# A hand-written planner for a gated MLP with a quantized down projection: how its orders are made and judged

## The chip, the cores and the metric

The kernel runs on one core of a Trainium2 chip. The metric is the device time of one execution in microseconds (us).

## The reference

For four sequences of 1,024 tokens with 512 features:

```python
scale = cond @ norm_w.T + 1.0
ms = jnp.mean(x * x, axis=-1, keepdims=True)
h = x * (scale[:, None, :] * jax.lax.rsqrt(ms + EPS))
u = h @ up_w.T                       # 512 -> 4096
val, gate = jnp.split(u, 2, axis=-1)
h = val * jax.nn.gelu(gate, approximate=False)
hq = act_quant(h)                    # per token: round(h * 127/max|h|), scaled back
wq = weight_quant(down_w)            # one scale: round(w / mean|w|) to -1, 0, 1
y = hq @ wq.T                        # 2048 -> 512
return y + x
```

The inputs are `x` (4, 1024, 512), `cond` (4, 128), `norm_w` (512, 128), `up_w` (4096, 512) and `down_w` (512, 2048), all float32.

## The kernel before

**The work.** A batch is one of the four sequences. For each batch the up projection goes over 16 blocks of 128 value and 128 gate features (`j`, or `g` counted through all batches); a block is a "slot". Weights and activations are split into a high and a low half in 16 bits, so that three matmuls make one product of 32-bit quality. Batch 0 is done block by block while the weights are still being loaded, scaled, transposed and split (`first_batch`, `plain_half`; matmuls on L886; the first of them in `plain_first`, L929). The weights also go in a rearranged form to a scratch tensor in device memory (`s_dram`). Batches 1 to 3 load them from there and use seven products of half-size blocks in place of eight (`slot`, `product`, L871), six matmuls of 512 columns to a product. The results of the products are collected in PSUM banks named A (two), B (one) and E (two), copied and combined by ScalarE (ACT: L949, L957, L961, gelu on L966 and L982; in batch 0 gelu on L910) and VectorE (DVE: L969, L979, L985, L988; in batch 0 L914).

**The down projection.** When a batch is up-projected, the maximum of each token is taken (DVE: L1005, L1007; then over partitions on GpSimd, POOL: L1021), turned into a scale (DVE: L1026, L1032), and the activations are scaled and rounded in pieces (DVE: L1063, L1067; ACT: L1071, L1075) during the next batch. Its matmuls (`Pair`, L1142; for the last batch `down_mm`, L1091) run in slots 10 to 13 of the next batch. They need four sums of weight blocks (`d_sums`, L771, DVE), and end in L1182 and L1100, which add `x` before the result is stored.

**The head.** The first loads, the rsqrt of the first token rows (L1214 to L1219), their scaling (L1224 on ACT, L1226 on DVE and POOL), their transposes on TensorE (PE, L1231), a table load for gelu on ACT (L1300), the maximum of the first weight rows (L578), a small matmul that spreads the condition (L482) and matmuls that only keep PE busy (`keep_warm`, L1247) are recorded in the order of the source.

**What sets the order.** Nothing above is issued at once. `Engine` records every call as a `Step` with its engine, a price in us and the steps it depends on (`Plan.add`); dependencies come from the memory that operands share. `Plan.order` then looks for an order in 24 rounds. In each, `needed` goes backwards and gives each step the latest time at which it may end (PE's steps are tied to their starts in the round before); `place` goes through the steps by that time and puts each in the first gap of its engine that is long enough (`Line`), except PE's, which are put one after the other; `replay` runs the resulting lists, each engine in order, against the prices and returns when PE is free. The round with the earliest end gives the order, and `emit` issues it; each engine then works strictly through its own list. DMAs are issued from the SP queue, a few from ACT. `price` holds the costs: a fixed part, a part per column, and for DVE and POOL a second, higher price for when the other of the two works at the same time.

Of the kernel before, what the change touches and what calls it, by code (L numbers as in the profile page):

```python
# [97 lines left out]
class Engine:  # L98
    def __init__(self, plan, name, real):
        self._plan, self._name, self._real = plan, name, real  # L100
# [10 lines left out]
class Plan:  # L111


    def __init__(self):
        self.steps = []
        self.wrote, self.read = {}, {}
        self.loaded = {}
        self.lines = {}

    def engines(self, nc):  # L120
# [3 lines left out]
    def add(self, eng, method, real, args, kwargs):  # L124
        s = Step()
        s.n, s.eng, s.do, s.args, s.kwargs = len(self.steps), eng, real, args, kwargs
        s.line = sys._getframe(2).f_lineno
        operands = [(i == 0, a) for i, a in enumerate(args)]
        operands += [(k in ("out", "accum_out"), a) for k, a in kwargs.items()]
        operands = [(w, a) for w, a in operands if isinstance(a, bass.AP)]  # L130
        writes = [a for w, a in operands if w]
        reads = [a for w, a in operands if not w]
        s.alone, s.beside, s.wait = price(eng, method, writes, reads, args, kwargs)
        deps = set()
        for v in reads:
            name, grains = _runs(v)
            wrote, read = self.wrote.setdefault(name, {}), self.read.setdefault(name, {})
            for g in grains:
                if g in wrote:
                    deps.add(wrote[g])  # L140
                r = read.setdefault(g, [])
                if r and r[-1] == s.n:
                    continue
                if eng == "PE" and r and self.steps[r[-1]].eng == "PE":
                    r[-1] = s.n
                else:
                    r.append(s.n)
        for v in writes:
            name, grains = _runs(v)
            wrote, read = self.wrote.setdefault(name, {}), self.read.setdefault(name, {})  # L150
            for g in grains:
                if g in wrote:
                    deps.add(wrote[g])
                deps.update(read.pop(g, ()))
                wrote[g] = s.n
        kind, s.before = None, 0.0
        if method == "activation" and args[2] in (AF.Sqrt, AF.Gelu):
            kind = args[2]
        elif eng == "POOL":
            kind = method == "partition_all_reduce"  # L160
        if kind is not None:
            was, members = self.loaded.get(eng, (None, []))
            if kind != was:
                deps.update(members)
                if eng == "POOL" and members:
                    s.before = RELOAD
                members = []
            elif members:
                deps.add(members[0])
            members.append(s.n)  # L170
            self.loaded[eng] = kind, members
        deps.discard(s.n)
        s.deps = deps
        self.steps.append(s)

    def order(self):

        steps = self.steps
        for s in steps:
            s.after, s.cost = [], (s.alone + s.beside) / 2  # L180
        for s in steps:
            for d in s.deps:
                steps[d].after.append(s)
        clock = 0.0
        for s in steps:
            if s.eng == "PE":
                s.start = clock
                clock += s.cost
        best = None
        for n in range(ROUNDS):  # L190
            self.needed(clock)
            self.place()
            order = sorted(steps, key=lambda s: (s.start, s.n))
            clock = self.replay(order)
            if best is None or clock < best[0]:
                best = clock, order
        self.replay(best[1])
        return best[1]

    def needed(self, clock):  # L200

        for s in reversed(self.steps):
            s.late = clock if s.eng != "PE" else s.start
            for t in s.after:
                s.late = min(s.late, t.late - lag(s, t) - s.wait - s.cost)

    def place(self):

        steps = self.steps
        used = {e: Line() for e in ("PE", "ACT", "DVE", "POOL", "SP", "DMA")}  # L210
        last = 0.0
        for s in sorted(steps, key=lambda s: (s.late, s.n)):
            t = max((steps[d].end + lag(steps[d], s) for d in s.deps), default=0.0)
            if s.eng == "PE":
                t = max(t, last)
                last = t + s.cost
                s.start, s.end = t, last
                continue
            s.start = used[s.eng].put(t - s.before, s.before + s.cost) + s.before
            s.end = s.start + s.cost  # L220
            if s.wait:
                s.end = used["DMA"].put(s.start + ISSUE, s.wait) + s.wait + LANDING

    def replay(self, order):

        steps = self.steps
        free = dict.fromkeys(("PE", "ACT", "DVE", "POOL", "SP", "DMA"), 0.0)
        port = {"DVE": 0.0, "POOL": 0.0}
        for s in order:
            e = s.eng  # L230
            t = free[e] + s.before
            for d in s.deps:
                t = max(t, steps[d].end + lag(steps[d], s))
            cost = s.alone
            if s.beside > s.alone:
                x = port["POOL" if e == "DVE" else "DVE"] - t
                if x > 0:
                    cost += (s.beside - s.alone) * min(1.0, x / s.alone)
                port[e] = t + cost
            s.start, s.end = t, t + cost  # L240
            s.cost = (s.cost + cost) / 2 if e in port else cost
            free[e] = s.end
            if s.wait:
                free["DMA"] = max(free["DMA"], t + ISSUE) + s.wait
                s.end = free["DMA"] + LANDING
        return free["PE"]

    def emit(self, steps):
        for s in steps:
# [2 lines left out]
            call(s.do, s.args, s.kwargs)  # L252


ROUNDS, ISSUE, LANDING, RELOAD = 24, 1.2, 1.5, 6.5


class Line:
# [17 lines left out]
def lag(s, t):  # L276

    if s.eng == t.eng:
        return 0.0
    if s.eng == "PE":  # L280
        return 0.2
    return 0.08 if t.eng == "POOL" else 0.05


def price(eng, method, writes, reads, args, kwargs):

    out = writes[0]
    n = _free(out)
    if "dma" in method:
        nbytes = n * out.shape[0] * mybir.dt.size(out.dtype)  # L290
        if "transpose" in method:
            return 0.45 + nbytes / 32768 * 0.16, 0.0, nbytes / 32768 * 0.17
        last = min(v.ap[-1][1] * mybir.dt.size(v.dtype) if v.ap[-1][0] == 1 else 4 for v in (out, reads[0]))
        return 0.45, 0.0, nbytes / (290e3 if last >= 1024 else 1.5e3 if last < 64 else 150e3)
    wide = max([n] + [_free(v) for v in reads if len(v.shape) > 1])
    psum = any(str(v.space).endswith("PSUM") for v in reads)
    if eng == "PE":
        f32 = any(v.dtype == F32 for v in reads)
        return (max(n, 64) * (2 if f32 else 1) / 2.4 + 2.5) / 1e3, 0.0, 0.0
    if eng == "ACT":  # L300
        cost = 0.06 + wide * 0.0009 + (0.07 if method != "copy" else 0)
        return cost, 0.0, 0.0
    if eng == "POOL":
        if method == "partition_all_reduce":
            return (1.8 if wide > 1 else 0.4), 0.0, 0.0
        if method == "tensor_scalar":
            cost = 0.2 + wide * 0.00092
            return cost, cost * 1.2, 0.0
        cost = 0.75 if wide <= 8 else 0.18 + wide * 0.00195
        return cost, cost * 1.33, 0.0  # L310
    if method == "reciprocal":
        return 0.17 + max(0, wide - 8) * 0.0056, 0.0, 0.0
    if wide <= 32:
        return 0.17, 0.0 if psum else 0.44, 0.0
    if psum or method in ("tensor_reduce", "memset"):
        return 0.1 + wide * 0.00108, 0.0, 0.0
    if method == "tensor_scalar":
        cost = 0.1 + wide * 0.00052
        return cost, cost * 2.2, 0.0
    if method == "tensor_tensor" and all(v.dtype in (BF16, F16) for v in reads):  # L320
        cost = 0.1 + wide * 0.00052
        return cost, cost * 1.6, 0.0
    cost = 0.1 + wide * 0.00106
    return cost, cost * (1.35 if method == "scalar_tensor_tensor" else 1.65), 0.0


class Rings:
# [1550 lines left out]
```

## Time and profile before

| | |
|---|---|
| median of 3 runs (lowest to highest) | 745.54 us (744.97 to 746.1) |
| the profiled execution: time, span | 746.14 us, 744.4 us |
| PE (matmuls) busy | 725.6 us |
| DVE busy | 606.1 us |
| ACT busy | 392.7 us |
| POOL busy | 210.5 us |
| mean granted TensorE clock | 0.998 |

The span goes from the first to the last instruction; the execution's own time has some start and end around it. A matmul counts as busy until its modelled end. An engine's idle time before an instruction is put down to what released that instruction.

### The profile page before, as it was taken

The numbers are of one execution on the slowest core, as the hardware profiler recorded it, in microseconds if no ns is written. First come the engines' busy times: TensorE is split into PE (matmuls) and PEld (weight loads), VectorE is DVE, ScalarE is ACT, GpSimd is POOL, SyncE is SP. The second block draws the span as 40 slices with busy tenths as digits, with TensorE's granted clock in tenths as the row PEclk, the third lists the DMA queues.
The fourth block names the chain that finished last, engine by engine and source line by source line (L and its number), as shares of the span: only waits on it lengthen the run. The fifth ranks groups of instructions, "written<-read, shape, count | busy, mean of one in ns | idle before, by whom it ended". The sixth has DMA issues, their size and how long they took to land.

```text
span 744.4 us, 10218 instructions
## 1 busy us (share of the span) xinstructions
PE 725.6 (97%) x3684; PEld 362.5 (49%) x3684; DVE 606.1 (81%) x833; ACT 392.7 (53%) x635; POOL 210.5 (28%) x213
## 2 busy tenths in 40 slices
PE   6999999999979999999999999999999999999997
PEld 3544444444434445666444445566444444445744
DVE  6787899988988887977587888988579889755897
ACT  5787576565225688333334678623333665332363
POOL 1775887857223034300015003800001000000000
PEclk9999999999999999999999999999999999999999
DMA  9838688899423454768733454676833344443514
GB/s 305 334 87 267 226 222 220 194 248 233 139 68 99 125 138 120 176 178 193 202 101 100 100 131 124 161 199 153 192 122 102 100 103 104 107 103 89 153 48 151
DMA packets 179567, 115.74 MB, mean 155 GB/s; under 512 B 141750, under 2 KB 147767, under 8 KB 179516
## 3 DMA queue, kind: packets, MB, share of 16 engines
q1 hardware_dynamic: 179226, 114.76, 57.5%
q10 hardware_dynamic: 290, 0.33, 0.3%
q8 instruction: 29, 0.48, 0.3%
q14 instruction: 22, 0.18, 0.1%
HBM read 58.93 MB, written 23.09 MB: 110 GB/s over the span
## 4 chain that ended last, share of the span: by engine, by line
PE 78%; DVE 9%; POOL 4%; issue 3%; ACT 3%; DMA 1%; SPq 0%; DVEq 0%; POOLq 0%; ACTq 0%
PE A L871 31%; PE E L871 15%; PE po L1142 8%; PE B L871 8%; PE E L886 5%; PE B L886 2%; PE A L886 2%; PE po L1091 2%; PE E L1091 1%; PE A L1091 1%; DMA H<-in_x_dram 1%; DVE H L629 1%; POOL H L663 1%; DVE nx L854 1%; DVE wam L578 1%
## 5 line engine op out<-in xcount | busy, mean ns | idle before, releaser
L871 PEld LDWEIGHTS <-SXY 128*128 128x128 f16 x2016 | 197.3, 98 | 237.1 <-issue 5.8
L871 PE MATMUL A<-R,SXY 128*128 128x512 f16 x1152 | 266.4, 379 | 3.7 <-ACT t L949 1.6
L871 PE MATMUL E<-R,SXY 128*128 128x512 f16 x576 | 140.0, 379 | 0.8 <-DVE t L979 0.8
L1021 POOL PARTITION_ALL_REDUCE am<-R x8 | 18.9, 2364 | 304.3 <-DVE R L1007 286.4
L1063 DVE TENSOR_TENSOR H<-H,am 128x1024 f32<-128x1024 f32 x64 | 78.3, 1256 | 0.2
L886 PEld LDWEIGHTS <-SXY 128*128 128x128 f16 x462 | 45.2, 98 | 55.6 <-issue 2.1
L969 DVE SCALAR_TENSOR_TENSOR H<-A,sg,t 128x512 f32<-128x512 f32 x48 | 35.9, 749 | 43.0 <-PE A L871 42.9
L871 PE MATMUL B<-R,SXY 128*128 128x512 f16 x288 | 70.0, 379 | 0.0
L1005 DVE TENSOR_REDUCE gm<-H 128x512 f32<-128x1024 f32 x56 | 69.0, 1232 | 1.0
L982 ACT ACTIVATE t<-t,sg 128x512 f32<-128x512 f32 x48 | 34.7, 722 | 54.6 <-DVE t L979 54.6
L949 ACT COPY t<-A 128x512 f32<-128x512 f32 x48 | 28.1, 585 | 60.0 <-PE A L871 60.0
L1142 PE MATMUL po<-wd,R 128*128 128x256 fp8e4 (+1 forms) x448 | 56.8, 275 | 0.8 <-ACT po L1168 0.8
L957 ACT COPY B<-A 128x512 f32<-128x512 f32 x48 | 27.4, 570 | 51.4 <-PE A L871 51.4
L1142 PEld LDWEIGHTS <-R 128*128 128x128 bf16 (+1 forms) x480 | 47.0, 98 | 13.9 <-issue 1.3
L985 DVE TENSOR_TENSOR v<-A,v 128x512 f32<-128x512 f32 x48 | 33.2, 691 | 24.9 <-PE A L871 22.4
L966 ACT ACTIVATE t<-B,sg 128x512 f32<-128x512 f32 x48 | 33.0, 687 | 32.6 <-PE B L871 32.0
L886 PE MATMUL E<-R,SXY 128*128 128x512 f16 x210 | 49.9, 379 | 0.0
L979 DVE TENSOR_TENSOR t<-E,t 128x512 f32<-128x512 f32 x48 | 33.0, 687 | 20.4 <-PE E L871 19.7
L886 PEld LDWEIGHTS <-R 128*128 128x128 f16 x282 | 27.5, 98 | 34.4 <-issue 2.0
L1071 ACT ACTIVATE H<-H 128x1024 f32<-128x1024 f32 x38 | 40.0, 1051 | 7.5 <-DVE H L1063 7.3
L961 ACT COPY v<-E 128x512 f32<-128x512 f32 x48 | 28.1, 586 | 28.4 <-PE E L871 21.5
L1007 DVE TENSOR_TENSOR R<-R,gm 128x512 f32<-128x512 f32 x56 | 40.4, 722 | 1.4
(232 smaller groups left out, 1036.9 us busy)
## 6 DMA issues: line engine op xcount, KB each, us to landing
SXY<-s_dram SPq DMA_DIRECT2D x66, 256.0 KB, 2.7
SXY<-s_dram SPq DMA_DIRECT2D x18, 384.0 KB, 3.9
H<-in_L_cond_up_w_dram SPq DMA_DIRECT2D x13, 512.0 KB, 5.5
s_dram<-SXY SPq DMA_DIRECT2D x14, 384.0 KB, 4.0
xr<-in_x_dram SPq DMA_DIRECT2D x19, 256.0 KB, 3.7
out_dram<-xr SPq DMA_DIRECT2D x19, 256.0 KB, 2.0
H<-in_x_dram SPq DMA_DIRECT2D x8, 512.0 KB, 5.3
R<-in_L_cond_down_w_dram SPq DMA_DIRECT2D x8, 512.0 KB, 7.4
```

What stands on the lines that cost most here:

```text
L871: PE.matmul(o, s[:, w, k, :], tv[:, :, c, l, k, :], start=start and n == 0, stop=stop and n == len(TERMS) - 1, skip_group_check=True,)
L886: PE.matmul(ps, a[k // 2][:, w, k % 2, :], XP[:, l, k, h * TOK : (h + 1) * TOK], start=n == 0, stop=n == len(terms) - 1,)
L966: ACT.activation(cur["t1"], pb, AF.Gelu, scale=gain(g, 1))
L969: DVE.scalar_tensor_tensor(h_half(g - 1, 0), prev["A"], gain(g - 1, 0), prev["t1"], ALU.mult, ALU.mult)
L979: DVE.tensor_tensor(prev["t2"], prev["E"], prev["t2"], ALU.add)
L982: ACT.activation(prev["t2"], prev["t2"], AF.Gelu, scale=gain(g - 1, 1))
L985: DVE.tensor_tensor(cur["v"], cur["A"], cur["v"], ALU.add)
L1005: DVE.tensor_reduce(gm[0], v, AX.X, ALU.max, apply_absolute_value=True)
L1007: return [largest, lambda: DVE.tensor_tensor(m, m, gm[0], ALU.max)]
L1063: DVE.tensor_tensor(v, v, r.to_broadcast([P, 2, TOK]), ALU.mult)
L1071: ACT.activation(v, v, AF.Copy, bias=MAGIC)
L1142: PE.matmul(po, w[:, j], m, start=start and j == 0, stop=stop and j == n - 1, skip_group_check=True,)
```

## The change

The instructions stay the same; only the planner and its prices are changed, and with them the order in which the instructions stand in each engine's list.

- `add`: each of the first 150 recorded steps that is not a DMA also depends on the step recorded before it on its engine, so these keep their recorded order (loads are free of it). Fifty-nine of them are PE's and 57 DVE's; they end in the first matmuls of `plain_first`.
- `order`: a round's order is replayed four more times with chance, and the mean of the four ends decides between 25 rounds; the margin that `place` gets goes round from 0 to 0.9 us.
- `needed`: a step without PE behind it must start, not end, a step's cost before the end.
- `place`: PE's steps may now go into any gap that fits, like those of other engines. The other engines' steps start later than their operands allow by up to the margin, but by no more than a tenth of their slack. A DMA from SP is issued when the DMA engines have room; one from ACT takes no room.
- `replay`: with chance, the cost of each step not on PE is multiplied by 0.95 to 1.09, and a DMA from SP lands up to 1 us later. It returns the end of the last step of all, not PE's.
- `price`: ACT's reads from PSUM cost 0.05 more and its base is changed; POOL's price beside DVE rises from 1.33 to 1.42 times, DVE's beside POOL from 1.65 to 1.8.

```diff
@@ class Plan
-        self.loaded = {}
+        self.loaded, self.last = {}, {}
...
+        if not s.wait:
+            if s.n < HEAD and eng in self.last:
+                deps.add(self.last[eng])
+            self.last[eng] = s.n
...
-        best = None
+        best, chance = None, random.Random(1)
         for n in range(ROUNDS):
             self.needed(clock)
-            self.place()
+            self.place(0.3 * (n % 4))
             order = sorted(steps, key=lambda s: (s.start, s.n))
             clock = self.replay(order)
-            if best is None or clock < best[0]:
-                best = clock, order
+            late = sum(self.replay(order, chance) for _ in range(MISSES)) / MISSES
+            if best is None or late < best[0]:
+                best = late, order
+            self.replay(order)
...
-            s.late = clock if s.eng != "PE" else s.start
+            s.late = s.start if s.eng == "PE" else clock - s.cost
...
-    def place(self):
+    def place(self, margin):
...
-        last = 0.0
         for s in sorted(steps, key=lambda s: (s.late, s.n)):
             t = max((steps[d].end + lag(steps[d], s) for d in s.deps), default=0.0)
-            if s.eng == "PE":
-                t = max(t, last)
-                last = t + s.cost
-                s.start, s.end = t, last
-                continue
+            if s.eng != "PE":
+                t += min(margin, max(0.0, s.late - t) * 0.1)
+            if s.wait and s.eng == "SP":
+                t = used["DMA"].put(t + ISSUE, s.wait) - ISSUE
             s.start = used[s.eng].put(t - s.before, s.before + s.cost) + s.before
-            s.end = s.start + s.cost
-            if s.wait:
-                s.end = used["DMA"].put(s.start + ISSUE, s.wait) + s.wait + LANDING
-
-    def replay(self, order):
+            s.end = s.start + (ISSUE + s.wait + LANDING if s.wait else s.cost)
+
+    def replay(self, order, chance=None):
...
+            if chance:
+                cost *= 1.0 if e == "PE" else 0.95 + 0.14 * chance.random()
+            else:
+                s.cost = (s.cost + cost) / 2 if e in port else cost
             s.start, s.end = t, t + cost
-            s.cost = (s.cost + cost) / 2 if e in port else cost
             free[e] = s.end
-            if s.wait:
+            if s.wait and e != "SP":
+                s.end = t + ISSUE + s.wait + LANDING
+            elif s.wait:
                 free["DMA"] = max(free["DMA"], t + ISSUE) + s.wait
-                s.end = free["DMA"] + LANDING
-        return free["PE"]
+                s.end = free["DMA"] + LANDING + (chance.random() if chance else 0.0)
+        return max(s.end for s in order)
...
-ROUNDS, ISSUE, LANDING, RELOAD = 24, 1.2, 1.5, 6.5
+HEAD = 150
+ROUNDS, MISSES, ISSUE, LANDING, RELOAD = 25, 4, 1.2, 1.5, 6.5
...
-        cost = 0.06 + wide * 0.0009 + (0.07 if method != "copy" else 0)
+        cost = 0.08 + wide * 0.0009 + (0.05 if method != "copy" else 0) + (0.05 if psum else 0)
...
-        return cost, cost * 1.33, 0.0
+        return cost, cost * 1.42, 0.0
...
-    return cost, cost * (1.35 if method == "scalar_tensor_tensor" else 1.65), 0.0
+    return cost, cost * (1.35 if method == "scalar_tensor_tensor" else 1.8), 0.0
```

More of the change, by code (lines that the diff above doesn't have):

```diff
@@ L1 @@
 import bisect
+import random
 import sys
```

## The prediction

> **What bounds the kernel now.** I read the page first: the span, and how much of it each engine is busy.
>
> ```profile
> span 744.4 us, 10218 instructions
> PE 725.6 (97%) x3684; PEld 362.5 (49%) x3684; DVE 606.1 (81%) x833; ACT 392.7 (53%) x635; POOL 210.5 (28%) x213
> ```
>
> TensorE is idle for 744.4 - 725.6 = 18.8 us. The change adds and removes no instruction: set side by side, the instruction lists of the two built programs hold the same entries on each engine (7,276 on PE with its weight loads, 829 DVE, 602 ACT, 223 POOL, 362 SP), in another order. So the question is what of the 18.8 us an order can take away. That the rest is full is seen in the chain that ended last, where a group of twelve matmuls of 512 columns reads
>
> ```profile
> 229.25 2.59 PE A L871 x12
> ```
>
> 2.59 / 12 = 0.216 us each, one behind the other. The windows view then places the idle time (columns: window; its us; busy us and count of PE, weight loads, DVE, ACT, POOL; granted clock; DMA share; GB/s):
>
> ```profile
> 0.00:20.00 20.00, 13.63 (x54) 6.77 (x54) 11.98 (x56) 10.31 (x21) 2.97 (x8) 0.91 0.92 312
> ...
> 140.00:160.00 20.00, 18.27 (x85) 8.21 (x84) 17.30 (x22) 11.62 (x20) 11.25 (x13) 1.00 0.99 239
> ...
> 200.00:220.00 20.00, 17.11 (x78) 7.51 (x77) 18.89 (x25) 6.34 (x13) 3.16 (x1) 1.00 0.28 80
> 220.00:240.00 20.00, 18.44 (x86) 8.30 (x85) 15.62 (x19) 11.75 (x17) 7.91 (x8) 1.00 0.36 98
> ...
> 720.00:744.40 24.40, 20.30 (x110) 10.58 (x108) 19.65 (x27) 10.46 (x10) 0.00 (x0) 1.00 0.37 130
> ```
>
> Idle: 6.37 in the first 20 us, 1.73 at 140, 2.89 + 1.56 = 4.45 at the change from batch 0 to batch 1, 4.10 at the end; 2.1 us are scattered. The list of PE's waits says who ended them (engine, line, releaser: total, times, longest):
>
> ```profile
> PE B L886 <- ACT t L910: 1.7, 1, 1.7
> PE A L871 <- ACT t L949: 1.6, 1, 1.6
> PE A L871 <- DVE v L985: 1.2, 1, 1.2
> ...
> PE A L886 <- ACT R L1235: 0.8, 4, 0.2
> PE po L1142 <- ACT po L1168: 0.8, 2, 0.5
> ```
>
> All of it is one engine's queue standing in the wrong order for PE, never a DMA in the main part.
>
> **The change part by part.** *The change of batch, 4.45 us.* DVE's timeline there:
>
> ```profile
> 191.93 2.35 DVE L771 TENSOR_TENSOR wd<-wd 128x1024 fp8e4<-128x1024 fp8e4 x2
> ...
> 196.86 3.20 DVE L771 TENSOR_TENSOR wd<-wd 128x1024 fp8e4<-128x1024 fp8e4 x2
> ...
> 201.09 3.39 DVE L1032 RECIPROCAL am<-am 128x128 f32<-128x128 f32 x4
> ...
> 206.52 0.68 DVE L985 TENSOR_TENSOR v<-A,v 128x512 f32<-128x512 f32 x1
> ...
> 215.04 0.63 DVE L979 TENSOR_TENSOR t<-E,t 128x512 f32<-128x512 f32 x1
> ```
>
> Four weight sums (L771), 2.35 + 3.20 = 5.55 us, stand in a queue that is already full, a good ten slots ahead of their use; then 215.04 - 206.52 = 8.5 us pass from slot 0's L985 to its L979, while PE has 36 matmuls for a slot, 36 x 0.216 = 7.8 us. In the new list the four sums stand about 60 places further back, in batch 1. Between L985 and L979 the new list has the scale L1026, the four reciprocals (3.39), one L969 and one L1063:
>
> ```profile
> L1063 DVE TENSOR_TENSOR H<-H,am 128x1024 f32<-128x1024 f32 x64 | 78.3, 1256 | 0.2
> L969 DVE SCALAR_TENSOR_TENSOR H<-A,sg,t 128x512 f32<-128x512 f32 x48 | 35.9, 749 | 43.0 <-PE A L871 42.9
> ```
>
> 3.39 + 1.26 + 0.75 = 5.4, and L1026, which is a pass over 512 columns and bounded by L985's 0.68, makes at most 6.1 us: under 7.8. I followed DVE, ACT and PE in this way, by hand and with such durations, over slots 0 to 4, and found no wait over 0.1 us. One thing there is still badly priced: the maximum over partitions on POOL, for which the planner still counts 1.8 us.
>
> ```profile
> 209.17 3.16 POOL L1021 PARTITION_ALL_REDUCE am<-R  x1 [9.42 <-DVE R L1007]
> ```
>
> DVE will stand for up to 3.16 - 1.8 = 1.4 us at L1026 of the second half, with an L969 queued behind it; PE wants the bank that this L969 frees only 18 matmuls, 3.9 us, after its input is complete, so I count nothing. Bounds: gain 4.45, or 4.45 - 1.4 = 3.05. I take 4.45.
>
> *The wait at 142, 1.73 us.* ACT and POOL there:
>
> ```profile
> 142.59 0.41 ACT L674 CAST R<-H 128x256 f16<-128x256 f32 x1 [4.60 <-POOL H L665]
> 142.90 0.68 ACT L910 ACTIVATE t<-B,sg 128x512 f32<-128x512 f32 x1
> ```
>
> The gelu (L910) that frees bank B stood behind a cast (L674) that waited 4.60 us for POOL. In the new list this gelu stands 12 places further forward and that cast 16 places behind it, so its input is the last thing it waits for. Gain 1.73; what could be late next is the gelu's own input, and that is complete three groups of twelve matmuls, 3 x 2.59 = 7.8 us, before the bank is wanted. If another late cast takes its place: 0.
>
> *The head.* The first 150 recorded steps now keep their order on each engine.
>
> ```profile
> 2.10 0.76 PE L482 MATMUL B<-H,one 1*128 1x128 f32 x2 [2.10 <-DMA H<-in_cond_dram]
> ...
> 13.19 0.55 PE L1231 MATMUL po<-ident,H 128*128 128x128 f32 x3 [2.74 <-DVE wam L456]
> ...
> 17.10 2.19 PE L929 MATMUL B<-R,SXY 128*128 128x512 f16 x6 [0.19 <-ACT SXY L638]
> ```
>
> ```profile
> 11.18 1.28 ACT L1300 ACT_TABLE_LOAD   x1
> ...
> 12.58 1.32 ACT L1224 ACTIVATE H<-H,rs 128x512 f32<-128x512 f32 x2
> ```
>
> ```profile
> 11.88 0.68 DVE L578 TENSOR_REDUCE wam<-H 128x1 f32<-128x512 f32 x1
> 12.47 0.66 DVE L1226 TENSOR_SCALAR H<-H,rs 128x512 f32<-128x512 f32 x1
> ```
>
> The scaling of the first x rows waits on DVE behind a maximum (L578), 12.47 - 11.88 = 0.59 us, and on ACT behind a table load until 12.58. In the new list L578 stands before the rsqrt chain, where DVE is idle, and the table load behind ten more ACT instructions. So the first transposes come 0.6 us earlier: gain 0.6. Against it: the load (12.58 - 11.18 = 1.40 us) now lies in the stretch where ACT converts weights, ahead of the cast that weight row 1 needs. Whether that cast then ends before PE asks for it hangs on fractions of a microsecond that the rows don't settle: cost taken 0, because ACT too starts 0.6 earlier and the weight copies that stood ahead of the cast go behind it; bounds 0 to 1.40. L482 goes behind three warm-up matmuls and the memset that they read; ACT wants its result only after the transposes of 13.19, so 0. The four waits of 0.2 on L1235 (0.8 in the list) come from casts ahead of it on ACT; in the new list the late one of them stands behind it: gain 0.8, bounds 0 to 0.8.
>
> *The end.*
>
> ```profile
> 740.03 0.27 PE L1091 MATMUL po<-wd,R 128*128 128x256 fp8e4 x1
> ...
> 740.23 0.48 DVE L1100 SCALAR_TENSOR_TENSOR R<-A,dq,R 128x256 f32<-128x256 f32 x1 [1.00 <-PE A L1091]
> 740.63 0.47 DVE L1100 SCALAR_TENSOR_TENSOR R<-po,dq,R 128x256 f32<-128x256 f32 x1
> ```
>
> The last piece waits 740.63 - 740.23 = 0.40 us on DVE behind the one before. In the new list bank A closes four matmuls before the end and not one, so this overlap goes: gain 0.3 (bounds 0 and 0.4). The rest of the 4.1 us, the last output's way out, stays.
>
> *Matmuls change places.* The products of six matmuls are no longer whole: the 2,016 L871 matmuls stand in 398 runs, not 336. Each of the 62 new joins may meet a copy that isn't done. The nearest row is the wait on L1168, 0.8 in 2, so 0.4 us each. A lower bound is 0, since PE is only sent elsewhere where the planner saw a gap; the upper bound 62 x 0.4 = 24.8. I take four such waits, 1.6 us, nearer to 0 because 336 runs end in the trace and the list of waits names five of their joins.
>
> *Sum*: -4.45 - 1.73 - 0.6 - 0.8 - 0.3 + 1.6 = -6.3 us. The profiled execution took 746.14 us, 1.74 more than its span; 746.14 - 6.3 = 739.8. It was the slowest of the three runs, 0.6 above their median of 745.54, so I forecast **739.2 us**.
>
> **The rivals.** *The clock stays up in the head.* Before 13.19 PE stands for 2.74 us, and then, with a granted clock of 0.51:
>
> ```profile
> 15.00:18.00 3.00, 2.81 (x12) 1.75 (x11) 2.30 (x6) 2.12 (x4) 1.22 (x2) 0.51 1.03 408
> ```
>
> The warm-up matmuls come later and the transposes 0.6 earlier, so the pause is 2.1 us or less. If the clock then stays full, the 2.81 us of PE work at half speed shrink by up to 1.4; 737.8. The Trainium skill ("TensorE: Matmul & The Clock Gate", Part 1) says that the clock is halved after an idle window of about 3.4 us, and that these windows run free of the kernel; by that rule a shorter pause is likelier to escape, and the time would be 737.8. The row agrees with it only as far as that a pause of 2.74 us was followed by half clock; how short is short enough, no row shows. Against the whole 1.4: half the head's work waits for DVE and ACT anyway. Chance 0.12.
>
> *The head gets worse.* ACT's 1.40 us of table load are exposed and the 0.6 and 0.8 don't come: 739.2 + 1.4 + 0.6 + 0.8 = 742.0. For it: the load's new place is where ACT feeds PE copy by copy. Chance 0.09.
>
> *Nothing is won.* The main part of the kernel in one row:
>
> ```profile
> 240.00:680.00 440.00, 439.24 (x2253) 220.19 (x2250) 350.15 (x445) 223.36 (x356) 65.64 (x63) 1.00 0.54 134
> ```
>
> The planner's model is as wrong in the new places as in the old: waits of the size of those removed (7.9 us less the 1.6 counted, 6.3) come up elsewhere; 745.5. For it: the same DVE work is only moved, into a part where DVE has 350.15 of 440 us already. Chance 0.10.
>
> *Slower.* The broken runs of matmuls meet late copies. It decides from 7.9 / 0.4 = 20 joins that wait; at 30, about half of the 62, the time is 745.5 + 10 x 0.4 = 749.5. Against it: in these 440 us PE stood for 0.76, although banks are reused as fast. Chance 0.14.
>
> **How the numbers follow.** Forecast 0.55. Faster by over 0.2% (1.5 us, about what a measurement of this kernel tells from no change): 0.55 + 0.12 + 0.09 = 0.76. Within: 0.10. Slower: 0.14. The range goes from the clock case without new joins (737.8 - 1.6 = 736.2, so 736.0) to past the case that nothing is won, 746.5; the slower case and a little below are left out.
>
> **What would show it.** Right: no PE wait over 0.5 us between 195 and 230, L771 on DVE well after 215; no wait on L910 near 140; first L929 at about 16.5; PE busy again near 725 in a span near 738. Wrong: PE waits of 0.2 to 0.5 on L949, L957, L969, L985 spread over the batches (the slower case); the first L886 later than 24.5 us (the head); a new wait over 1 us where DVE's L771 now stand.

## The result, and the profile after

The kernel after took 736.26 us (median of 4 runs, 735.99 to 738.3), the kernel before beside it 745.47 us: a ratio of 0.9882, with a 95% interval of 0.9863 to 0.9901. The forecast was 739.2, the range 736.0 to 746.5. The profiled execution took 735.99 us with a span of 734.1; before, it was 746.14 and 744.4. So the change brought 9 to 10 us where 6.3 were forecast.

The page after, its first lines:

```profile
span 734.1 us, 10201 instructions
PE 722.8 (98%) x3684; PEld 362.1 (49%) x3684; DVE 606.9 (83%) x833; ACT 392.3 (53%) x635; POOL 217.0 (30%) x213
```

TensorE's (PE's) idle time fell from 18.8 to 11.3 us, its busy time by 2.8 us (the prediction's sign had it stay near 725). The windows view after, in the stretches shown of before:

```profile
0.00:20.00 20.00, 14.03 (x60) 6.71 (x61) 12.29 (x58) 10.38 (x22) 3.15 (x8) 1.00 0.78 249
140.00:160.00 20.00, 20.00 (x94) 9.05 (x93) 19.12 (x22) 13.86 (x24) 17.20 (x20) 1.00 1.03 229
200.00:220.00 20.00, 20.00 (x94) 9.05 (x93) 17.88 (x24) 8.24 (x15) 4.43 (x3) 1.00 0.49 154
220.00:240.00 20.00, 20.00 (x94) 9.09 (x93) 17.10 (x21) 11.90 (x17) 7.78 (x7) 1.00 0.43 106
720.00:734.10 14.10, 10.49 (x63) 5.91 (x61) 9.71 (x16) 4.12 (x4) 0.00 (x0) 0.98 0.44 158
```

PE is full in the three windows that held 1.73 and 4.45 us of idle time. The list of PE's waits has nothing over 1.15 us behind the head (L1258 and L1242 are in the head; lines are 11 higher than before):

```profile
PE A L1258 <- DVE eps L1198: 3.6, 1, 3.6
PE po L1153 <- DVE xr L1193: 1.1, 1, 1.1
PE po L1242 <- DVE wam L467: 1.1, 1, 1.1
PE B L940 <- ACT SXY L649: 0.7, 1, 0.7
PE E L897 <- DVE H L925: 0.5, 1, 0.5
```

VectorE's (DVE's) timeline at the change of batch:

```profile
198.29 0.69 DVE L996 TENSOR_TENSOR v<-A,v 128x512 f32<-128x512 f32 x1 [0.69 <-PE A L882]
...
205.14 0.69 DVE L990 TENSOR_TENSOR t<-E,t 128x512 f32<-128x512 f32 x1 [0.22 <-PE E L882]
...
211.68 0.43 DVE L1037 TENSOR_SCALAR am<-am 128x512 f32<-128x512 f32 x1 [0.70 <-POOL am L1032]
...
253.64 2.36 DVE L782 TENSOR_TENSOR wd<-wd 128x1024 fp8e4<-128x1024 fp8e4 x2
```

From L996 to L990 of one slot now pass 205.14 - 198.29 = 6.85 us, under the 7.8 that PE needs for a slot, where it was 8.5; the first weight sums (L782) stand at 253.64. Beside each other, the same matmul starts in the two traces at:

| | before | after | gained in the stretch |
|---|---|---|---|
| first main matmul (L929, L940) | 17.10 | 16.13 | 0.97 |
| first of the second block (L886, L897) | 24.52 | 23.27 | 0.28 |
| first matmul of batch 1 (L871, L882) | 195.51 | 190.69 | 3.57 |
| a bank-B product behind the change of batch | 227.79 | 217.89 | 5.08 |
| end of the last matmul | 740.30 | 730.49 | -0.09 |
| end of the span | 744.4 | 734.1 | 0.49 |

The first two rows hold more than the change: in the profiled execution of the kernel before, the granted clock was 0.51 between 15 and 18 us, and other executions with the same head don't show that (see b_warm).

### The profile page after: what moved, and what is told of

Same layout as the page of the kernel before. It is cut to its first block, busy times and chain, and to the rows that moved or that the text cites. A ratio compares the mean times of both kernels' runs of the same rounds, so it can differ in the third digit from the quotient of the medians.

```text
span 734.1 us, 10201 instructions
## 1 busy us (share of the span) xinstructions
PE 722.8 (98%) x3684; PEld 362.1 (49%) x3684; DVE 606.9 (83%) x833; ACT 392.3 (53%) x635; POOL 217.0 (30%) x213
## 4 chain that ended last, share of the span: by engine, by line
PE 89%; DMA 4%; DVE 3%; ACT 2%; issue 0%; POOL 0%; SPq 0%
PE A L882 34%; PE E L882 17%; PE B L882 8%; PE po L1153 8%; PE E L897 8%; PE B L897 4%; PE A L897 4%; DMA rows_dram<-scT 2%; PE po L1102 2%; PE E L1102 1%; PE A L1102 1%; DMA s_dram<-R 1%; DMA H<-in_x_dram 1%; DMA am<-in_x_dram 1%; PE B L1153 0%; ACT R L1218 0%
## 5 line engine op out<-in xcount | busy, mean ns | idle before, releaser
L882 PEld LDWEIGHTS <-SXY 128*128 128x128 f16 x2016 | 197.2, 98 | 229.4 <-issue 1.4
L882 PE MATMUL A<-R,SXY 128*128 128x512 f16 x1152 | 270.4, 379 | 0.0
L882 PE MATMUL E<-R,SXY 128*128 128x512 f16 x576 | 142.9, 379 | 0.0
L1032 POOL PARTITION_ALL_REDUCE am<-R x8 | 17.3, 2158 | 249.8 <-DVE R L1018 249.8
L897 PEld LDWEIGHTS <-SXY 128*128 128x128 f16 x462 | 45.1, 98 | 53.5
L882 PE MATMUL B<-R,SXY 128*128 128x512 f16 x288 | 70.8, 379 | 0.0
L1153 PE MATMUL po<-wd,R 128*128 128x256 fp8e4 (+1 forms) x448 | 59.0, 275 | 0.0
L990 DVE TENSOR_TENSOR t<-E,t 128x512 f32<-128x512 f32 x48 | 33.0, 688 | 24.0 <-PE E L882 23.6
L786 POOL TENSOR_SCALAR ssq<-ssq 128x2 f32<-128x2 f32 x12 | 4.8, 397 | 154.1 <-ACT H L816 113.0
L897 PE MATMUL E<-R,SXY 128*128 128x512 f16 x210 | 49.6, 379 | 0.0
L996 DVE TENSOR_TENSOR v<-A,v 128x512 f32<-128x512 f32 x48 | 33.1, 690 | 19.4 <-PE A L882 17.7
L1018 DVE TENSOR_TENSOR R<-R,gm 128x512 f32<-128x512 f32 x56 | 44.4, 793 | 0.8
L897 PEld LDWEIGHTS <-R 128*128 128x128 f16 x282 | 27.6, 98 | 33.0 <-issue 0.7
```

Of the source, the lines that this page charges most:

```text
L882: PE.matmul(o, s[:, w, k, :], tv[:, :, c, l, k, :], start=start and n == 0, stop=stop and n == len(TERMS) - 1, skip_group_check=True,)
L897: PE.matmul(ps, a[k // 2][:, w, k % 2, :], XP[:, l, k, h * TOK : (h + 1) * TOK], start=n == 0, stop=n == len(terms) - 1,)
L990: DVE.tensor_tensor(prev["t2"], prev["E"], prev["t2"], ALU.add)
L996: DVE.tensor_tensor(cur["v"], cur["A"], cur["v"], ALU.add)
L1018: return [largest, lambda: DVE.tensor_tensor(m, m, gm[0], ALU.max)]
L1153: PE.matmul(po, w[:, j], m, start=start and j == 0, stop=stop and j == n - 1, skip_group_check=True,)
```

## The experiments

The kernels whose names begin with b are the kernel before with one edit, those with a the kernel after. Where an order was edited, it was the finished list, with every dependency kept.

**b_sums: before, with only the weight sums moved on DVE.**

```diff
 L914
-L771 x2
 L914, L1005, L1007
-L771 x2
...
 L985, L988
+L771
 L1118 x2
...
```

> The kernel before, with only its eight weight sums (L771 on DVE) moved: the four that stood in the change of batch go to places after 267 us, the list is otherwise as it was. Theory (a wait of PE costs its idle time and about 0.16 us more, since a matmul is 0.379 us long but the next one starts 0.216 us after it): the waits of 4.45 us between 200 and 240 us go, with four to five of these additions, 745.5 - 5.1 = 740.4 us, and PE is busy for at least 19.8 of the 20 us in both windows. Rival (the change of batch is full anyway, the next late step takes over): at least half of the 4.45 us stays, 743 us or more. Rival (the gain comes from the clock in the head): 745.5 us.

Measured: 742.59 us against 745.65, ratio 0.9957 (0.9944 to 0.9970). The windows:

```profile
200.00:220.00 20.00, 19.50 (x91) 8.77 (x90) 16.23 (x21) 9.35 (x17) 7.70 (x6) 1.00 0.40 103
220.00:240.00 20.00, 20.00 (x95) 9.08 (x93) 17.63 (x21) 12.52 (x17) 3.66 (x4) 1.00 0.33 98
240.00:300.00 60.00, 58.48 (x295) 28.66 (x294) 53.67 (x64) 42.87 (x72) 23.57 (x24) 1.00 0.49 123
```

The sums were the cause at the change of batch: 3.95 of the 4.45 us of idle time go (one window reads 19.50, under the 19.8 that was written). But 1.52 us come back where the sums now stand, from 253.1 us on, in a stretch in which PE had been busy all 60 us. So their time seems not to have been free in DVE's queue there; the kernel after rearranged what stands around it as well.

**b_swap: before, with the gelu ahead of the cast on ScalarE (ACT).**

```diff
-L674 R<-H
 L910 t<-B
+L674 R<-H
```

> The kernel before, with one pair on ACT swapped: the gelu L910 that frees bank B at 142 us is issued ahead of the cast L674 that waits for POOL. Theory: the one wait of 1.73 us goes with its 0.16 us, 745.5 - 1.9 = 743.6 us. Rival (another step of ACT or POOL is late behind it, since the cast is now a gelu later): less than 0.9 us, 744.6 to 745.5 us.

Measured: 745.50 us, ratio 0.9997 (0.9989 to 1.0006): nothing. PE's timeline shows where the wait went:

```profile
151.86 2.75 PE L886 MATMUL B<-R,SXY 128*128 128x512 f16 x12 [0.52 <-ACT t L910]
155.55 2.75 PE L886 MATMUL E<-R,SXY 128*128 128x512 f16 x12 [0.94 <-DVE H L914]
```

The wait of 1.73 us at 143 is gone, and 0.52 and 0.94 us come 9 and 12 us later. DVE's L914 frees bank E at 154.76 behind three subtractions and a rounding step:

```profile
150.49 1.22 DVE L629 TENSOR_TENSOR H<-H 128x1024 f16<-128x1024 f32 x1
151.62 2.08 DVE L854 TENSOR_TENSOR nx<-xn,nx 128x512 f16<-128x512 f32 x2
153.63 1.21 DVE L749 TENSOR_SCALAR R<-R 128x1024 f32<-128x1024 f32 x1
154.76 0.74 DVE L914 SCALAR_TENSOR_TENSOR H<-E,sg,t 128x512 f32<-128x512 f32 x1
```

Here the rival holds: PE's earlier wait had hidden the lateness of the next two steps.

**b_warm: before, with the pause ahead of the first transposes filled.**

```diff
 L1247 (matmul that keeps PE busy) x7
+L1247 x11
 L1231 (first transpose)
```

> The kernel before with eleven more matmuls that only keep PE busy, behind the seven that stand ahead of the first transposes (L1247), so that the pause of 2.74 us becomes one of about 0.4 us; nothing else is changed. If the pause is what brings the clock down: the granted clock is 1.00 between 15 and 18 us, the first L929 comes 0.5 to 1.0 us earlier, and the time is 744.5 to 745.0 us. If all of the 1.4 us of half speed counts: 744.1 us. If the clock falls without regard to the pause: it is near 0.5 for some 3 us as before, and the time is 745.5 us.

Measured: 745.94 us, ratio 1.0006 (0.9994 to 1.0017). The windows view of the profiled execution, and PE's first main matmul:

```profile
15.00:18.00 3.00, 2.10 (x15) 1.20 (x13) 2.62 (x7) 2.52 (x5) 1.14 (x2) 1.00 1.03 409
```

```profile
16.70 0.39 PE L929 MATMUL B<-R,SXY 128*128 128x512 f16 x1 [0.71 <-ACT SXY L638]
```

The clock stayed at 1.00 and L929 came 0.40 us earlier than in the profile of before, not 1.4, since it then waits 0.71 us for ACT. But this isn't the edit's doing. b_sums and b_swap have the head of the kernel before unedited; in their profiles the pause was 2.06 and 1.54 us, the clock 1.00 from 13 to 20 us, and L929 started no later (b_sums first):

```profile
16.61 0.39 PE L929 MATMUL B<-R,SXY 128*128 128x512 f16 x1 [0.71 <-ACT SXY L638]
16.46 0.39 PE L929 MATMUL B<-R,SXY 128*128 128x512 f16 x1 [0.71 <-ACT SXY L638]
```

The half clock in the head belongs to the one execution of before that was profiled. Its mean clock was 0.998; of the 25 executions of before timed beside b_warm, 24 had 0.999 or 1.000. So this run can't show what the pause does to the clock, and there was next to no lost clock in the head for the change to win back. In the whole time of b_warm no gain is to be seen either. The clock in the head isn't what the change brought.

**a_sums_early: after, with four sums moved back.**

```diff
 L1016, L1018
+L782 x2
 L1016, L1018
+L782 x2
 L1016, L996
...
-L782 x2
...
-L782 x2
```

> The kernel after, with the first four weight sums (L782 on DVE) moved back into the change of batch, two behind each of two L1018 at about 191 and 193 us. Theory: PE waits there again for 3.5 to 4.5 us, and the time is 736.3 + 4 to 5 = 740.3 to 741.3 us. Rival (the free order of the matmuls, or the other moves on DVE, take up the delay): within 1 us of the kernel after, 736.3 to 737.3 us.

Measured: 743.09 us, 6.8 above the kernel after. PE's timeline, and the granted clock in the windows behind it:

```profile
202.98 0.62 PE L882 MATMUL A<-R,SXY 128*128 128x512 f16 x2 [4.10 <-DVE v L996]
```

```profile
202.00:204.00 2.00, 1.02 (x4) 0.47 (x4) 1.97 (x4) 0.00 (x0) 0.00 (x0) 0.85 0.01 3
204.00:206.00 2.00, 2.00 (x7) 0.65 (x5) 2.00 (x4) 0.00 (x0) 0.00 (x0) 0.50 0.00 0
206.00:208.00 2.00, 2.00 (x9) 0.85 (x8) 0.69 (x1) 0.69 (x1) 0.00 (x0) 0.79 0.40 87
```

The wait is the expected one, and above it comes what wasn't expected: behind 4.10 us without work the clock falls to 0.50. In these three windows of 2 us, with clocks of 0.85, 0.50 and 0.79, PE loses about 0.3 + 1.0 + 0.4 = 1.7 us. The run doesn't restore the place that the sums had before: there the two pairs started 3.6 us ahead of the batch's first matmul and 1.4 behind it, here 3.6 and 7.7 behind it (193.85 and 197.99 against 190.30). It shows that sums in this stretch stop PE, not what before's cost.

**Undoing one rule of the planner at a time.** Each of these lets the planner find another order under the remaining rules.

```diff
a_nohead:   -HEAD = 150
            +HEAD = 0
a_pefixed:  +        last = 0.0
            ...
            -            if s.eng != "PE":
            +            if s.eng == "PE":
            +                t = max(t, last)
            +                last = t + s.cost
            +            else:
a_nochance: -            late = sum(self.replay(order, chance) for _ in range(MISSES)) / MISSES
            -            if best is None or late < best[0]:
            -                best = late, order
            -            self.replay(order)
            +            if best is None or clock < best[0]:
            +                best = clock, order
a_nomargin: -            self.place(0.3 * (n % 4))
            +            self.place(0.0)
```

> The kernel after, with HEAD = 0: the recorded order of the first 150 steps no longer binds, everything else as after. In its new list the table load for gelu and the maximum L589 stand again ahead of the scaling, as in the kernel before; the weight sums stay late. If the head's order is worth the 0.97 us that the first main matmul came earlier: 737.3 us, with the first L940 at about 17.1 us. If the head decides the whole gain: near 745 us. If it is worth nothing beyond the noise of the head: 736.3 us.

> The kernel after, with PE's steps placed one behind the other in order of due time, as before (no broken runs of matmuls); everything else as after. The weight sums stay late. Theory (the gain comes from the order on DVE and ACT, the matmuls' freedom is not its source): 735.3 to 737.3 us, with 336 runs of L882 again. Rival (matmuls that change places fill the gaps): 739 us or more, with waits of PE in the change of batch.

> The kernel after, but each round is judged by its plain replay, as before, and not by replays with chance; margins, prices, head and free matmuls as after. The round that it picks is another one, with two weight sums early in the change of batch. Theory (the judge decides which order is used, and so what PE waits for): PE waits 1 to 4 us between 190 and 240 us, 738 to 742 us. Rival (margins and prices do it, any round is good): 736.3 us within 1.

> The kernel after, but no room is left behind operands (the margin is 0 in every round); judged with chance, prices, head and free matmuls as after. All eight weight sums stand late in its list too. If the room is what keeps small lateness from PE: waits of 0.2 to 1 us spread over the batches, 738 to 741 us. If the place of the weight sums is all that counts: 736.3 us within 1.

| | median us | ratio to before (95%) | PE's largest waits behind the head, us |
|---|---|---|---|
| after | 736.26 | 0.9882 (0.9863 to 0.9901) | 1.15, 0.46 |
| a_pefixed | 739.54 | 0.9925 (0.9910 to 0.9940) | 1.88 at 102, 1.18 at 483 |
| a_nohead | 744.03 | 0.9976 (0.9966 to 0.9985) | 4.00 at 82 |
| a_nochance | 745.15 | 0.9991 (0.9976 to 1.0006) | 3.17 at 85, 1.45 at 81 |
| a_nomargin | 748.00 | 1.0043 (1.0025 to 1.0061) | 2.99 at 80, 2.49 at 204, 1.10 at 218 |

Most of these expectations failed. All four lose, by 3 to 12 us, and hardly where expected: a_nochance is full to 0.24 us in the change of batch although two sums stand early, and a_nomargin waits there although all stand late. Each is another order from end to end, so the times don't price the rule that was undone. a_nochance also loses by the clock: its two runs at a mean of 0.998 took 742.0 and 742.2 us, the nine at 0.991 to 0.995 took 743.7 to 748.0. What the four share is a wait of PE for bank E, `E L897 <- DVE H L925`, between 80 and 102 us (in a_nochance the same lines are two lower, in a_pefixed four higher). It is the longest in each behind the head, though a_nomargin loses more in all, 3.66 us, in the change of batch. In a_nohead this is PE's, DVE's and SP's timeline:

```profile
82.47 1.02 PE L897 MATMUL E<-R 128*128 128x512 f16 x4 [4.00 <-DVE H L925]
```

```profile
78.47 1.22 DVE L589 TENSOR_REDUCE wam<-H 128x2 f32<-128x1024 f32 x1 [4.55 <-DMA H<-in_L_cond_up_w_dram]
...
81.68 0.74 DVE L925 SCALAR_TENSOR_TENSOR H<-E,sg,t 128x512 f32<-128x512 f32 x1
```

```profile
68.51 0.33 SPq L556 DMA_DIRECT2D sc<-rows_dram  x1
68.89 0.78 SPq L808 DMA_DIRECT2D am<-in_x_dram  x1
69.77 0.41 SPq L581 DMA_DIRECT2D H<-in_L_cond_up_w_dram  x1
```

The maximum over new weight rows (L589) waits 4.55 us for their load; L925, which frees PE's bank E, is queued behind it on DVE. The load was issued behind two others. (In a_nomargin L925 stands behind a subtraction that waits 2.15 us for ACT; there and in the other two no run shows what made L925 late.) Part of a_nohead's loss is in the head itself: its first L940 starts at 18.23 us, 2.1 later than after's, behind a pause of 3.72 us and with the clock at 0.50.

**a_nohead_load: that load moved ahead.**

```diff
 L551 x2, L693
+L581 H<-in_L_cond_up_w_dram
 L556 sc<-rows_dram
 L808 am<-in_x_dram
-L581 H<-in_L_cond_up_w_dram
```

> a_nohead with one DMA moved in SP's list: the load of weight rows (L581) that lands at 78.4 us is issued ahead of the two loads (L556, L808) it stood behind, the first of which held SP from 61.8 to 68.5 us. Nothing else is changed. Theory (PE's wait of 4.00 us at 82 us comes from that load's place, by way of the maximum L589 that holds up L925 on DVE, and it brings the clock down behind it): the wait goes, with its 0.16 us and some 1.5 us of lower clock; 744.0 - 5.7 = 738.3 us, and DVE waits for the load no more than 1 us. Rival (the DMA engines are full there, another load then comes late): 742 us or more.

Measured: 740.71 us, 3.3 below a_nohead, with a ratio of 0.9929 (0.9912 to 0.9947). DVE no longer waits for the load, and the 4.00 us are gone; PE is busy for 39.03 us between 60 and 100, where it was 36.00. One new wait, 0.96 us on ACT's L921 at 89 us, takes some of it back, and the pause in the head was 0.6 longer in its profile. So the load's place is the cause, and its worth was put 2.4 us too high. The load was issued only 0.9 us earlier (68.87 us, before 69.77), yet L589 could start at 74.23 and not at 78.47: what counts is what no longer stands ahead of it in SP's list.

**a_round21: after's rules, the next choice.** The judge may not take round 1, whose order the kernel after uses.

```diff
-            if best is None or late < best[0]:
+            if n != 1 and (best is None or late < best[0]):
```

> The kernel after, except that round 1, whose order it uses, may not be chosen; the judge then takes round 21, with the same margin of 0.3 us, and also with late weight sums. If the replays with chance rank orders well: 736.5 to 738 us. If the order of the kernel after was a lucky one among equals: 739 us or more, with one or two waits of 1 to 4 us at places where the kernel after has none.

Measured: 755.73 us, ratio 1.0127 (1.0107 to 1.0147): 10 us slower than the kernel before. It is the case of the lucky order, but with a wait far longer than the 1 to 4 us written for it. PE's, DVE's and SP's timeline:

```profile
87.48 1.86 PE L897 MATMUL E<-R 128*128 128x512 f16 x4 [11.15 <-DVE H L925]
93.22 1.87 PE L897 MATMUL E<-R 128*128 128x512 f16 x4 [3.87 <-DVE H L925]
```

```profile
83.03 1.22 DVE L589 TENSOR_REDUCE wam<-H 128x2 f32<-128x1024 f32 x1 [16.01 <-DMA H<-in_L_cond_up_w_dram]
```

```profile
58.54 0.43 SPq L551 DMA_DIRECT2D rows_dram<-scT  x1
59.05 0.46 SPq L693 DMA_DIRECT2D s_dram<-R  x1
59.62 0.37 SPq L581 DMA_DIRECT2D H<-in_L_cond_up_w_dram  x1
60.04 1.03 SPq L551 DMA_DIRECT2D rows_dram<-scT  x1
```

The same chain as in a_nohead, but L589 gets its rows only 83.0 - 59.6 = 23.4 us after the load's issue. The next such load, issued at 67.5 us, landed after 21.5; in the kernel after the median of the thirteen is 4.3 us, the longest 10.8. Around the late load stand two stores of 2 KB in pieces of 4 bytes (L551). (One of the eight weight sums ran at 182.2 us, not late as written; PE has no wait in the change of batch.)

**a_round21_small: those two stores moved away.**

```diff
-L551 rows_dram<-scT
+L551 rows_dram<-scT x3
 L808, L556
-L551 rows_dram<-scT
 L693, L581
-L551 rows_dram<-scT
```

> a_round21 with two DMAs moved in SP's list: the second and third store of the condition's rows (L551, 2 KB each in pieces of 4 bytes), which stood at 58.5 and 60.0 us around a load of weight rows (L581, 59.6 us), are issued right behind the first of them at 46.8 us, as the kernel before has them. All else is a_round21's. Theory (the small stores keep the DMA engines from the load, which landed 23.4 us after its issue, and so hold up L589, L925 and PE for 11.15 and 3.87 us): both waits go but for 1 us at most, with their lower clock of 2 to 3 us; 737 to 740 us. Rival (the load is late behind the large stores L693 or for lack of room in the tile): the waits stay over 5 us, 748 us or more.

Measured: 739.49 us, ratio 0.9915 (0.9900 to 0.9931), 16.2 below a_round21. No wait of PE on L925 is left, and the longest of DVE for such a load is now

```profile
62.17 1.22 DVE L589 TENSOR_REDUCE wam<-H 128x2 f32<-128x1024 f32 x1 [2.32 <-DMA H<-in_L_cond_up_w_dram]
```

which PE doesn't feel. The place of the small stores was the cause. The large stores (L693) weren't: they still stand on both sides of the load, at 63.0 and 64.1 us with the load at 63.5.

**a_best: after, with two places of DVE's list changed.**

```diff
-L604, L925
+L925, L604
...
-L865, L1193 x2
+L1193 x2, L865
```

> The kernel after with two places of DVE's list changed: two stores' sums L1193 ahead of the subtraction L865 at 490.6 us, and L925 ahead of the small L604 at 76.3 us. If a wait costs its idle time and 0.16 us: the waits of 1.15 and 0.46 us go, 736.2 - 1.9 = 734.3 us. If other steps become late there, as in b_swap: 735.5 to 736.3 us.

Measured: 735.41 us, ratio 0.9875 (0.9848 to 0.9901), 0.85 below the median of the kernel after; the intervals of the two overlap, so the ratios alone don't tell them apart. The runs at full clock do (four of a_best at a mean of 0.999 or 1.000: 734.1 to 735.5 us; three of after: 736.0 to 736.3), and so do the profiles: the profiled span is 732.7 us against 734.1, and the windows that held the two waits went from 39.54 and 158.85 us of PE work to

```profile
60.00:100.00 40.00, 39.95 (x191) 18.79 (x190) 35.33 (x49) 27.66 (x45) 35.80 (x32) 1.00 0.71 185
400.00:560.00 160.00, 160.00 (x852) 83.18 (x851) 131.86 (x168) 85.00 (x139) 39.95 (x35) 1.00 0.60 146
```

A wait of 0.29 us came up at 223, which accounts for part of what is missing to the 1.9 expected.

## Why the prediction was right, and where it was not

**The change of batch** was the right step with the right cause. The term was 4.45 us, measured 5.08. The missing part is the price of a wait: a matmul of 512 columns counts as busy for 0.379 us, but the next one follows after 0.216 (twelve take 2.75 us by the timeline, and the next twelve start 2.59 behind), so a wait costs its idle time and another 0.16 us. Four waits: 4.45 + 0.65 = 5.1. The trace after shows all that was named for this step: L996 to L990 in 6.85 us (6.1 us were counted for what stands between them, and L996 itself comes on top), the wait for the maximum of 0.70 us (up to 1.4), and PE without a wait. b_sums shows the sums as the cause in the kernel before; a_sums_early shows that sums in this stretch stop PE in the kernel after too.

**The wait at 142** went, but not for the reason given. "What could be late next is the gelu's own input" was the step that failed: b_swap made just that exchange, and the next late steps, L910 and DVE's L914, took 1.46 of the 1.73 us. In the kernel after the whole stretch is in another order, and only there the wait is gone without an heir. A wait in one engine's queue was priced without asking for how long the other queues had been late behind its cover.

**The head** was forecast at 0.6 us. The two profiles give 0.97 to the first main matmul and 1.25 to the second block. But beside the same head at full clock, in b_sums and b_swap (first L929 at 16.61 and 16.46, first L886 at 23.68 and 23.52), it is 0.33 to 0.48 and 0.25 to 0.41: under the forecast. The rest, 0.8 to 1.0 us, is the half clock of one execution, which is also why the profiled times lie 10.15 us apart and the medians 9.21. So the rival of the clock took a trait of that execution for one of the kernel, and its 1.4 us weren't there to be won. The table load was covered, as taken: PE waits for ACT's L649 0.68 us, as it waited for the same step, L638, 0.71 us in b_sums.

**The four waits of 0.2** on L1235 cost 0.8 + 4 x 0.16 = 1.4 us, forecast 0.8, and the wait of 0.5 on L614 (in the list of before), which no term named, went too, about 0.7 us. With the 1.9 at 142, and less 0.9 for two new waits of 0.15 and 0.46, this is 3.1 of the 3.57 us of the table's third row; what the other 0.5 was isn't known.

**The new joins** were put at +1.6 us and cost nothing that the trace shows: no matmul on L882 is in the list of waits after. This term is the farthest off. From 240 us to the last matmul the two traces keep step within 0.1 us: the only wait of size is the 1.15 us on L1193, and before's on L1168 (0.76) are gone. **The end** brought 0.49 us, forecast 0.3.

**In sum**, the 6.3 us of the forecast, the 1.6 of the joins and 0.16 for each of the nine waits that were counted make 6.3 + 1.6 + 1.4 = 9.3; the medians lie 9.2 apart, and the smaller misses nearly cancel. The measured time is 0.26 us above the lower end of the range. That end had been set by the case of the clock without new joins; that the range held is in part luck.

**Of the rivals**, "slower" needed 20 joins that wait, and there were none to speak of. But a slower kernel was nearer than the 0.14 that it got: the planner's rules as such don't make the kernel faster. a_round21 keeps every one of them but for the choice of the round, and is 1.3% slower than before. The prediction didn't forecast the rules; it followed one finished order, in the change of batch slot by slot, and that is why its largest term came out right. Its sentence "never a DMA in the main part" was true of PE's waits in the trace and so hid what decided two of the five other orders, a_nohead and a_round21: none of its terms and rivals has the SP queue, whose order the change also alters (a DMA is placed by when the engines have room).

What stays open: why the order of round 1 keeps clear of the late load, and what makes L925 late in the other three orders. That the planner counts the small stores as shorter than they are isn't shown by any run; no run changed a DMA's price alone.

## What to carry to other kernels

Judge a scheduler's change by the order that it gives, not by its rules, and try the next order that it would have chosen: two orders found under the same rules lay 19 us apart. Before a wait is counted as gain, ask how late the next two steps on the other queues are behind its cover; swap the pair alone to see. Before a profile's clock is taken as the kernel's, look at a second execution. Look for tiny scattered stores ahead of loads that a busy queue waits for.

## What the runs showed of the hardware

A DMA of 2 KB in 4-byte pieces took 12.2 us to land (the median in the kernel after), and 13.2 and 14.3 in a_round21_small and a_round21. Loads issued beside it in a_round21 came late, and between 64 and 72 us the DMA engines there read as busy and move little (windows view; the last two columns are share and GB/s):

```profile
64.00:68.00 4.00, 4.00 (x25) 2.33 (x23) 3.02 (x4) 0.00 (x0) 1.27 (x2) 1.00 0.96 38
68.00:72.00 4.00, 4.00 (x20) 1.83 (x19) 0.00 (x0) 0.00 (x0) 0.00 (x0) 1.00 0.99 60
```

The Trainium skill ("DMA: Bandwidth & Descriptors", Specifications) says that transfers below 512 bytes don't reach line rate; these rows agree, at 38 and 60 GB/s against 312 in the first 20 us of the kernel before. With the stores moved away (a_round21_small), the same two windows read a share of 0.88 and 0.90 at 321 and 344 GB/s. The share is rough in short windows (of 2 us: from 0.35 to 1.64 in the same stretch), so that the small stores hold the engines themselves is likely but not shown; that their place made the load late is.

The clock fell to 0.50 in or behind pauses of PE of 4.10 us (a_sums_early), 4.00 and 3.72 (a_nohead), 11.15 (a_round21) and 2.99 (a_nomargin). Pauses of 2.49 (a_nomargin), 2.06 (b_sums) and 1.88 us (a_pefixed) left it at 1.00; one of 2.11 (b_warm) and one of 1.71 in the head of a_round21_small were followed by it. Of the latter's six runs three had a mean clock of 0.995 and took 740.4 to 740.5 us, and three 1.000 and 737.5 to 738.6: the same kernel, 2.4 us apart. The Trainium skill ("TensorE: Matmul & The Clock Gate", Part 1) says that the clock halves after an idle window of about 3.4 us and that the windows run free of the kernel. The long pauses agree with it; that one of 2.11 us can be enough, and one of 1.71 with a gap of 0.33 and transposes behind it, means that a window needn't be wholly idle, or that something else counts, such as what PE does between the gaps, which no run here separates.
